# Layer 1 of a two-layer graph attention kernel: tile 29 of head 0 through logarithms, tile 28 of its sum through a DMA

## The chip, the cores and the metric

The kernel runs on one core of one Trainium2 chip. The metric is the device time of one execution in microseconds (us); the median of three executions of the kernel before is 2761.76 us (2758.8 to 2762.07).

## What is computed

Two graph layers are applied to x (4096 x 512, fp32) with one 4096 x 4096 adjacency matrix of zeros and ones. The change is in layer 1 alone:

```python
data1 = (h @ W.T + b).reshape(4096, 8, 64)         # h = relu(layernorm(x)), 8 heads of 64
src, trg = sums of data1 * src_proj, data1 * trg_proj over the 64 columns
e = src.T[:, :, None] + trg.T[:, None, :]          # 8 x 4096 x 4096
e = where(e >= 0, e, 0.01 * e) + adj
out = softmax(e, axis=-1) @ data1 (per head);  x = x + out
```

Layer 1 adds the adjacency matrix to the scores, so every pair of nodes takes part. The kernel writes a weight as max(z, g) times d times exp(adj), with a factor z of each output row and head and two factors g and d of each neighbour and head; the weights of a head, summed over the neighbours, are its softmax denominator.

## The kernel before, in words

Layer 0 and the linear part of layer 1 come first and are not touched. Layer 1's attention (lines 1232 to 1614) then runs over 8 groups: 4 blocks of 1024 output rows times 2 sets of 4 heads (k = 0 to 3). A group runs over 32 tiles m of 128 neighbours. For every tile and head a product tile `pr[i, m, k]` of 128 x 1024 is made, and TensorE multiplies it with the values.

**Products.** VectorE makes each by one scalar_tensor_tensor (L1379 for head 0, L1382 for the others; order 3, 0, 1, 2). ScalarE supplies exp(adj) once per tile (`exps`, L1319, one buffer `ex`), head 3's own factor (`last_exps`, L1329) and head 0's relu (`relus`, L1355). Tiles in `BY_LOG` are different for head 0: ScalarE writes a relu of logarithms into the single buffer `lg_row` (`logs`, L1335, four tiles ahead), GpSimd adds the adjacency tile to it in two halves (`add_logs`, L1344: the first half in the step of tile m-2, the second in that of m-1, held back behind head 3's product there), and ScalarE's exponential of it is the product itself (`relus`, L1352). VectorE then has three products for that tile in place of four. Head 0's products have three buffers in turn, those of head 3 two.

**Denominators.** Heads 1 and 2: four matmuls per tile (`den`). Head 3: GpSimd adds the products up (L1393) and TensorE sums the result over the partitions in the last tile. Head 0: each tile goes one of two ways. Those in `BY_DMA` are added by an accumulating DMA from GpSimd's queue into one of two accumulators `acc[i, 0, 0]`, `acc[i, 0, 1]` in turn (L1365; tiles 0 and 1 are copied in at L1363); the turn is counted so that tile 30 lands in the second. Those in `BY_HALF` are split: TensorE sums the left half at once by one matmul (L1447), and GpSimd adds the right half into `acc[i, 0, 2]` (L1397, L1399). In `gather` (L1401), the last tile brings in the accumulators: acc[i,0,0] and acc[i,3] right after the values of heads 3 and 0, then acc[i,0,2], and at the very end acc[i,0,1] (L1450).

**TensorE's columns.** Matmuls of layer 1 use 32 of the array's 128 columns, so that four stand side by side, one in each column group 0 to 3. A tile has 20 of them, five per column group. `n`, the number of `BY_HALF` tiles before m modulo 4, sets with which group a tile begins (`cols`), and the left half's matmul of a `BY_HALF` tile goes to group n. While a group of tiles runs, `finish` turns the results of the group before at tiles 2, 6, 10 and 14 (L1499), always beginning with column group 0.

**Order.** Each engine runs its instructions in the order in which the program text issues them; `stages` (L1596) sets how many tiles each function is ahead of `gather`. In the step of a tile, `weigh` (L1367) issues on GpSimd's queue: the DMA of the tile before (`sums`), the second half of the logarithms of tile m+1, head 3's add, the first half of the logarithms of tile m+2, and the half sum.

Of the kernel before, what the change touches and what calls it, by code (L numbers as in the profile page):

```python
# [28 lines left out]
def kernel(  # L29
# [657 lines left out]
    def slot(name):  # L687
        n = taken.get(name, 0)
        taken[name] = n + 1
        return slots[name][n % len(slots[name])]  # L690
# [544 lines left out]


    PARTS = (0, 1, 2, 4, 5, 6, 8, 9, 10, 12, 13, 14, 16, 17, 18, 22)
    BY_LOG = (3, 7, 11, 15, 19, 23, 27, 31)
    BY_HALF = (4, 8, 12, 16, 20, 24, 28)
    BY_DMA = [m for m in range(NT - 1) if m not in BY_HALF]  # L1240
    after = mybir.DependencyInfo(mybir.DependencyClass.Sync, mybir.DependencyReason.DATA)

# [3 lines left out]
    with tile_pool("rl") as rlp, tile_pool("zb") as zp1, tile_pool("ac") as acp, tile_pool("s1") as sp, tile_pool(  # L1246
# [85 lines left out]
        def logs(i, m, early=False):  # L1332
            if m in BY_LOG and early == (m == BY_LOG[0]):
                r = lg_row
                nc.scalar.activation(r, us[i], AF.Relu, bias=nlg_m[:, groups[i][1], m:m + 1], scale=-(1.0 - SLOPE))  # L1335
                rl[i, m] = r

        def early_logs(i, m):
            logs(i, m, True)

        def add_logs(i, m, half, behind=None):
            if m in BY_LOG:
                cs = slice(half * BL, (half + 1) * BL)
                add = nc.gpsimd.tensor_tensor(rl[i, m][:, cs], rl[i, m][:, cs], ra[i, m][:, cs], ALU.add)  # L1344
                if behind is not None:
                    tc.add_manual_dep(add.ins, behind.ins.name, after, reason="behind head 3's product")

        def relus(i, m):
            h = groups[i][1] * HG
            if m in BY_LOG:  # L1350
                pr[i, m, 0] = slot("pr0")
# [15 lines left out]
        def weigh(i, m, order=ORDER):  # L1367
# [26 lines left out]
            add_logs(i, m + 2, 0)  # L1394
            if m == BY_HALF[0]:
                acc[i, 0, 2] = acp.tile([P, BL], FP, name="acc02", bufs=1)
                nc.gpsimd.tensor_copy(acc[i, 0, 2], pr[i, m, 0][:, BL:])  # L1397
            elif m in BY_HALF:
                nc.gpsimd.tensor_tensor(acc[i, 0, 2], acc[i, 0, 2], pr[i, m, 0][:, BL:], ALU.add)  # L1399

        def gather(i, m):  # L1401
# [5 lines left out]
            v, dn = pv[i]  # L1407
            n = sum(u < m for u in BY_HALF) % 4
            cols = [(n + c) % 4 for c in range(4)]
# [13 lines left out]
            def ones(col, row, src, stop=False):  # L1423
                den(col, zo[:, 3 - row:4], src, start=False, stop=stop)

            def halves(src):
                return [src[:, q * BL:(q + 1) * BL] for q in range(HV)]
# [13 lines left out]
            for col in cols:  # L1441
# [3 lines left out]
                    start=(m == 0), stop=(last and r == 1))  # L1445
            if m in BY_HALF:
                ones(n, 3 if n else 1, halves(pr[i, m, 0])[0])  # L1447
# [149 lines left out]
        for s in range(len(steps)):  # L1597
            for f, ahead in stages:
                if s + ahead < len(steps):
                    f(*steps[s + ahead])  # L1600
                if s == 0 and f is exps:
                    early_logs(0, BY_LOG[0])
            if s == 0:
# [45 lines left out]
```

## Time and profile before

| | |
|---|---|
| median of three executions | 2761.76 us |
| the profiled execution | 2753.08 us, of which the profile's span is 2751.3 us |
| TensorE clock granted, mean | 0.999 |
| layer 1's attention | some 1180 us of the span; a group takes 146.4 us |

In a group of 146.4 us, TensorE is busy for all of it, VectorE for 145.7 us, GpSimd for 125.3 us and ScalarE for 120.8 us. The profile calls TensorE's matmuls PE and its weight loads PEld, VectorE DVE, ScalarE ACT, GpSimd POOL and SyncE, which loads the adjacency tiles, SP. A line "L1382 DVE ... he_t<-z,rm,ex" is an instruction of line 1382 that writes a buffer in tile he_t from z, rm and ex; buffers of layer 0 are used again under their old names, so that head 0's product is called he_t or pr, and head 3's he_t for an even tile and at for an odd one. A fp32 matmul shows as two records. "[0.40 <-DVE ...]" is idle time before an instruction and what ended it.

### The profile page before, as it was taken

Reading aid. Unit: us, or ns where it says so; the run is one execution under the profiler, and the core shown is the slowest. Engines: PE = TensorE matmul, PEld = TensorE weight load, DVE = VectorE, ACT = ScalarE, POOL = GpSimd, SP = SyncE. Lnnn points to the kernel's source line nnn. Section 1 sums busy time; section 2 is a strip of 40 time slices with the busy share of each in tenths; the row PEclk is TensorE's granted clock in tenths of the full one; section 3 lists DMA queues with packets and bytes.
Section 4 is the critical chain, followed back from the end, with each engine's and each line's share of the span. In section 5 each row is a group of like instructions: output and inputs, shape, how many; then the busy total and the mean of one; then the engine's idle time right before and its main releaser. Section 6 shows DMA issues by size and latency. Waiting matters only on the chain.

```text
span 2751.3 us, 49011 instructions
## 1 busy us (share of the span) xinstructions
PE 2733.0 (99%) x17839; PEld 1774.7 (65%) x17839; DVE 2473.0 (90%) x3362; ACT 1545.5 (56%) x2498; POOL 1454.8 (53%) x1252
## 2 busy tenths in 40 slices
PE   8999999999999999999999999999999999999999
PEld 6885444446888888888885433565656565655555
DVE  6767789899989888888886799999999999999998
ACT  6422233333133333433433588988788888888886
POOL 5313434453011011101108588988889897979797
PEclk9999999999999999999999999999999999999999
DMA  6628898888999999999866589999999999989897
GB/s 207 190 68 298 280 328 302 312 300 262 216 212 197 196 263 204 229 257 228 232 193 166 172 203 263 226 223 242 234 240 221 242 234 241 228 241 230 218 221 173
DMA packets 537122, 632.10 MB, mean 230 GB/s; under 512 B 292184, under 2 KB 346488, under 8 KB 536880
## 3 DMA queue, kind: packets, MB, share of 16 engines
q1 hardware_dynamic: 463600, 419.28, 50.5%
q0 software_dynamic: 71776, 206.81, 34.9%
q8 instruction: 140, 2.29, 0.3%
q10 hardware_dynamic: 1504, 2.88, 0.3%
q14 instruction: 102, 0.84, 0.1%
HBM read 406.33 MB, written 107.15 MB: 187 GB/s over the span
## 4 chain that ended last, share of the span: by engine, by line
PE 80%; DVE 7%; DMA 3%; issue 3%; SPq 3%; POOL 2%; ACT 2%; DVEq 0%; POOLq 0%; ACTq 0%
PE pv L1416 28%; PE po L845 21%; PE pe L585 12%; PE dn L1421 8%; PE bank L297 6%; SPq L768 2%; PE po L980 2%; DVE he_t L1382 2%; DMA et<-er_d 1%; PE pt L1499 1%; DMA a<-in_adj_t_dram 1%; POOL a L992 1%; PE bank L230 1%; PE bank L237 0%; DVE at L812 0%
## 5 line engine op out<-in xcount | busy, mean ns | idle before, releaser
L1416 PE MATMUL pv<-he_t,sup 128*32 128x512 f32 x6488 | 988.0, 592 | 1.1 <-DVE he_t L1382 1.1
L1416 PEld LDWEIGHTS pv<-he_t,sup 128*32 128x32 f32 x6488 | 434.9, 110 | 311.4 <-issue 110.7
L1421 PE MATMUL dn<-he_t,acc_z 128*2 128x512 f32 x1984 | 412.9, 592 | 0.0
L585 PE MATMUL pe<-he_t,he_t 128*128 128x512 f32 x896 | 386.2, 592 | 0.0
L802 ACT ACTIVATE d<-d 128x1024 f32<-128x1024 f32 x126 | 133.3, 1058 | 423.2 <-DVE d L794 223.4
L1319 ACT ACTIVATE ex<-he_t 128x1024 f32<-128x1024 f32 x255 | 262.3, 1029 | 148.1 <-DVE he_t L1382 147.0
L1393 POOL TENSOR_TENSOR acc<-acc,at 128x1024 f32<-128x1024 f32 x120 | 287.9, 2399 | 69.9 <-DVE at L1382 63.7
L1382 DVE SCALAR_TENSOR_TENSOR he_t<-z,rm,ex 128x1024 f32<-128x1024 f32 x256 | 315.3, 1271 | 0.5
L1382 DVE SCALAR_TENSOR_TENSOR he_t<-he_t,rm,ex 128x1024 f32<-128x1024 f32 x254 | 312.8, 1271 | 0.8 <-PE dn L1421 0.4
L585 PEld LDWEIGHTS pe<-he_t,he_t 128*128 128x128 f32 x896 | 169.3, 190 | 210.3 <-issue 193.8
L1393 POOL TENSOR_TENSOR acc<-acc,he_t 128x1024 f32<-128x1024 f32 x120 | 287.5, 2396 | 26.6 <-DVE he_t L1382 26.6
L1416 PE MATMUL pv<-at,sup 128*32 128x512 f32 x1024 | 279.7, 593 | 0.0
L845 PE MATMUL po<-sup,ux 128*128 128x256 f32 x1024 | 263.3, 379 | 0.0
L845 PE MATMUL po<-he_t,at 128*128 128x256 f32 x1024 | 263.0, 379 | 0.1
L845 PE MATMUL po<-sup,at 128*128 128x256 f32 x1024 | 242.4, 380 | 1.3 <-DVE at L812 1.1
L845 PEld LDWEIGHTS po<-sup,at 128*128 128x128 f32 x1024 | 194.0, 190 | 29.5 <-DVE at L812 3.4
L845 PEld LDWEIGHTS po<-he_t,at 128*128 128x128 f32 x1024 | 194.3, 190 | 27.3 <-ACT zs L875 0.5
L845 PEld LDWEIGHTS po<-sup,ux 128*128 128x128 f32 x1024 | 193.9, 190 | 26.1
L812 DVE TENSOR_TENSOR at<-d,a 128x1024 f32<-128x1024 f32 x126 | 154.1, 1223 | 62.7 <-PE po L845 30.9
L596 ACT ACTIVATE nr<-rm 128x1 f32<-128x1 f32 x144 | 29.3, 204 | 301.5 <-DVE rm L587 290.6
L590 POOL DMA_DIRECT2D er_d<-mk x136 | 75.3, 553 | 226.2 <-DVE rm L587 214.1
L1416 PE MATMUL pv<-pr,sup 128*32 128x512 f32 x680 | 187.7, 592 | 0.0
(349 smaller groups left out, 5345.6 us busy)
## 6 DMA issues: line engine op xcount, KB each, us to landing
he_t<-in_adj_t_dram SPq DMA_DIRECT2D x256, 512.0 KB, 6.3
acc<-he_t POOLq DMA_DIRECT2D x127, 512.0 KB, 6.8
a<-in_adj_t_dram SPq DMA_DIRECT2D x126, 512.0 KB, 5.3
acc<-pr POOLq DMA_DIRECT2D x65, 512.0 KB, 6.4
ac<-in_adj_t_dram SPq DMA_DIRECT2D x124, 256.0 KB, 4.9
ar<-in_adj_dram SPq DMA_DIRECT2D x120, 256.0 KB, 4.6
ec_d<-mc POOLq DMA_DIRECT2D x120, 256.0 KB, 5.0
er_d<-mk POOLq DMA_DIRECT2D x112, 256.0 KB, 4.5
```

The costliest lines, as they stand in the source:

```text
L297: nc.tensor.matmul(acc[:, j, :], w, m, start=(k == 0), stop=(k == KC // 2 - 1))
L585: nc.tensor.matmul(pe[:, :w], he_t[i][:, k, (t % TB) * P:(t % TB + 1) * P], he_t[j][:, k, BL - w:], start=(k == 0), stop=(k == KC - 1))
L590: nc.gpsimd.dma_start(er_d[rows, lo + sk:lo + w], mk[:, sk:w])
L768: nc.sync.dma_start(e[c * S:(c + 1) * S, h, 0:r * P].rearrange("p (a q) -> p a q", q=S), sq[c])
L802: nc.scalar.activation(d, d, AF.Exp)
L812: nc.vector.tensor_tensor(w, d, aj.pop((n, q)), ALU.mult)
L845: nc.tensor.matmul(acc[:, j, :], A[:, j * P:(j + 1) * P], B, start=(first_ and j == 0), stop=last, skip_group_check=True)
L1319: nc.scalar.activation(x_, ra.pop((i, m)), AF.Exp)
L1382: p_ = nc.vector.scalar_tensor_tensor(w, zs_[i, k], g_m[:, h + k, m:m + 1], e3.pop((i, m)) if k == 3 else x_, op0=ALU.max, op1=ALU.mult)
L1393: nc.gpsimd.tensor_tensor(acc[i, 3], acc[i, 3], w, ALU.add)
L1416: nc.tensor.matmul(v[c][q][col * Q:(col + 1) * Q, :], va[:, m, g * HG + k, c0:c0 + Q], pr[i, m, k][:, q * BL:(q + 1) * BL], start=(m == 0) ...
L1421: nc.tensor.matmul(dn[col * Q:col * Q + w.shape[1], :], w, src, **fl)
```

## The change

```diff
     PARTS = (0, 1, 2, 4, 5, 6, 8, 9, 10, 12, 13, 14, 16, 17, 18, 22)
-    BY_LOG = (3, 7, 11, 15, 19, 23, 27, 31)
-    BY_HALF = (4, 8, 12, 16, 20, 24, 28)
+    BY_LOG = (3, 7, 11, 15, 19, 23, 27, 29, 31)
+    BY_HALF = (4, 8, 12, 16, 20, 24)
     BY_DMA = [m for m in range(NT - 1) if m not in BY_HALF]
```

In each of the 8 groups, tile 29's head 0 loses VectorE's product and ScalarE's relu and gets ScalarE's relu of logarithms, two half adds on GpSimd and ScalarE's exponential. Tile 28's head 0 loses the left half's matmul on TensorE and the right half's add on GpSimd and gets an accumulating DMA of 128 x 1024. `BY_DMA` grows from 24 to 25 tiles, so the turn of the two accumulators starts the other way round: tile 2 is added to the accumulator into which tile 1 was copied, no longer to that of tile 0; from tile 27 on, tiles 28 and 30 go to the second and 27 and 29 to the first. Tiles 29 to 31 begin with TensorE's column group 2 in place of 3. In the changed program the exponentials of tiles 29 and 31 wait for the landing of a DMA besides GpSimd's halves, which that of tile 31 did not before: their buffers were last used by tiles 26 and 28, which now are both read by a DMA. No other line is changed.

## The prediction

> **What bounds the kernel now.** I read first the busy times by window, since the page's shares are means over two layers. This is a whole group of 32 tiles of layer 1, then three stretches at its end and the next one's start (columns: window, its length, busy time and instructions of each engine, granted clock, DMA share, GB/s).
>
> ```profile
> 2422.80:2569.20 146.40, 146.40 (x1477) 85.30 (x1473) 145.71 (x122) 120.75 (x142) 125.34 (x83) 1.00 0.93 234
> 2430.00:2435.00 5.00, 5.00 (x53) 3.15 (x47) 5.00 (x5) 3.35 (x4) 4.44 (x3) 1.00 0.70 265
> 2435.00:2440.00 5.00, 5.00 (x52) 3.10 (x48) 5.00 (x6) 3.39 (x4) 4.43 (x3) 1.00 0.94 195
> ...
> 2445.00:2450.00 5.00, 5.00 (x52) 3.04 (x46) 5.00 (x6) 4.43 (x7) 1.66 (x2) 1.00 1.03 376
> ```
>
> Two engines look full: TensorE with 146.40 us and VectorE with 145.71. Busy shares can't say which one sets the pace. The starts of the matmuls can (timeline of TensorE, tiles 27, 29 and 31, whose head 3 is in at):
>
> ```profile
> 2424.26 0.60 PE L1416 MATMUL pv<-at,sup 128*32 128x512 f32 x2
> ...
> 2432.85 0.60 PE L1416 MATMUL pv<-at,sup 128*32 128x512 f32 x2
> 2433.28 0.60 PE L1416 MATMUL pv<-at,sup 128*32 128x512 f32 x2
> ...
> 2441.43 0.60 PE L1416 MATMUL pv<-at,sup 128*32 128x512 f32 x2
> ```
>
> Records of one column group follow each other every 0.43 us (2432.85, 2433.28), so a matmul of two records holds its group for 0.858 us, and a tile of five per group takes 4.29 us. Tiles 29 and 30 take 2441.43 - 2432.85 = 8.58 us, exactly twice that: **TensorE runs without a gap**. The waits of five groups (who waited for whom; us in total, times, longest) say the same:
>
> ```profile
> PEld pv L1416 <- DVE he_t L1382: 2.9, 9, 0.4
> ...
> ACT he_t L1352 <- POOL lg L1344: 15.0, 26, 0.6
> ...
> DVE he_t L1382 <- PE dn L1421: 0.2, 1, 0.2
> ```
>
> TensorE waits 0.6 us per group for products, and VectorE's whole idle time is 146.4 - 145.7 = 0.7 us. VectorE's lead over TensorE is widest in the middle of a group and falls to 2441.43 - 2439.92 = 1.5 us at tile 31 (end of its head 3, below). TensorE sets the pace; VectorE is close behind.
>
> The Trainium skill's page "Perfetto Trace Analysis", section "Identifying the Most-Contended Engine", warns that matmul busy time doesn't measure how close TensorE is to its limit, and would take VectorE's occupancy of 99.5% as the bound; by it, the sum below would be VectorE's term, -3.9 to -9.5 us. The spacing of the matmuls speaks for TensorE.
>
> **The change, part by part, per group.**
>
> *TensorE: one matmul less (tile 28, column group 2).* Shared by four groups it would be 0.858 / 4 = 0.21 us, at most 0.858 us. But tiles 27 and 28, with it, took 2432.85 - 2424.26 = 8.59 us, as long as tiles 29 and 30 without. Column groups run on independently and meet again where the results are turned (tile 14) and after the last tile. In between, the half sums of tiles 16, 20, 24, 28 lie on groups 3, 0, 1, 2, and the last tile puts 2, 3, 2, 2 more matmuls on groups 0 to 3. That makes 3, 4, 3, 3; without tile 28's, 3, 4, 2, 3. Group 1 is the longest in both. I take **0**; the end for the range is 8 x -0.858 = -6.9 us.
>
> *VectorE: one product less (tile 29).* Its row is 1.27 us, from start to start 1.19 us; 8 x 1.19 = 9.5 us at most. What replaces it runs on ScalarE and GpSimd, both in order, so I walk the group's end with the timeline's rows, GpSimd's (head 3's add of tile 27, the half sum of tile 28 that goes, head 3's add of tile 31), ScalarE's (logarithms of tile 31, `ex` of tile 29) and VectorE's (tile 29's heads 3 and 0, tile 31's head 3):
>
> ```profile
> 2421.87 2.40 POOL L1393 TENSOR_TENSOR acc<-acc,at 128x1024 f32<-128x1024 f32 x1 [0.42 <-DVE at L1382]
> ...
> 2427.87 1.28 POOL L1399 TENSOR_TENSOR acc<-acc,pr 128x512 f32<-128x512 f32 x1
> ...
> 2440.08 2.40 POOL L1393 TENSOR_TENSOR acc<-acc,at 128x1024 f32<-128x1024 f32 x1 [0.45 <-DVE at L1382]
> ```
>
> ```profile
> 2427.27 1.14 ACT L1335 ACTIVATE lg<-racc,mb 128x1024 f32<-128x1024 f32 x1
> 2428.96 1.03 ACT L1319 ACTIVATE ex<-he_t 128x1024 f32<-128x1024 f32 x1 [0.55 <-DVE he_t L1382]
> ```
>
> ```profile
> 2428.85 1.39 DVE L1382 SCALAR_TENSOR_TENSOR at<-z,rm,he_t 128x1024 f32<-128x1024 f32 x1
> 2430.16 1.27 DVE L1379 SCALAR_TENSOR_TENSOR he_t<-rl,mb,ex 128x1024 f32<-128x1024 f32 x1
> ...
> 2438.60 1.32 DVE L1382 SCALAR_TENSOR_TENSOR at<-z,rm,he_t 128x1024 f32<-128x1024 f32 x1
> ```
>
> The relu of tile 29's logarithms (1.14) goes behind tile 27's exponential, where ScalarE waits 1.05 us for VectorE: free. On GpSimd, head 3's add of tile 27 ends at 2424.2; the first half (1.28) ends at 2425.5, the DMA issue (0.85) at 2426.3, the second half at 2427.6. Tile 29's exponential (1.15 for the relu's 1.23) can then start at 2427.7, not 2426.1; the relu of tile 31 follows until 2429.9 and `ex` of tile 29 runs 2429.8 to 2430.8, **0.84 us later than now**. VectorE, done with head 3 at 2430.2, waits 0.6 us for it. So of 1.19 us about **0.5 us** stays; tile 30's products start at 33.24, not 33.73. In groups 0 and 1 ScalarE also scales values (0.57 per tile) and nothing stays. All of it lies behind TensorE, which reads these products 1.5 us and more later: I take 0; the end is -9.5 us.
>
> *GpSimd:* two halves more (2 x 1.28), one less (1.28) and a DMA issue (0.85): +2.1 of 21 us of idle time. Continuing the walk: head 3's add of tile 28 ends at 2430.0, the new DMA of tile 28 is issued until 2430.8, tile 29's add ends at 33.25, tile 31's halves at 34.5 and 36.6 (now 36.5), tile 31's add at 42.2 (now 42.5). TensorE reads it at 2443.2. Hidden; uncovered it would cost what it is late.
>
> *Exponentials of tiles 29 and 31* now wait for landings of the DMAs of tiles 26 and 28. Tile 26's, issued at 2420.58, took 6.0 us, landing 2426.6, before 2427.7. Tile 28's, issued at 2430.0 with 5.6 to 7 us, lands between 2435.6 and 2437, against 2436.6 for the halves. At most 0.4 us late; ScalarE's copies of the results, for which the next group's first matmul (2447.6) waits, end at 2447.1 now and would end about 0.5 earlier. Hidden.
>
> *Tile 2's add* goes to the accumulator that tile 1 is being copied into. That copy landed 0.6 to 1.6 us after the add's issue in groups 1 to 7 (2457.91 against 2457.32 here), and GpSimd stands for that long; queued behind are head 3's add and tile 3's DMA. Three operations later GpSimd idles 1.81 us. VectorE's product of tile 5, which reuses tile 2's buffer, starts at 2466.90, and that DMA landed at 2464.39. Hidden; else up to 7 x 1.6 us.
>
> *One accumulating DMA of 512 KB more.* The window 2430 to 2435 has room (share 0.70), those after it less (0.94 to 1.03). What matters is tile 30's DMA, in TensorE's way at 2446.80: issued at 2438.79, landed at 2445.01 after 6.2 us. Over the groups this slack is 1.45 to 2.05 us. Six DMAs would now follow each other, 4.5 us apart, where there were three; the last of three at 3.6 us took 6.8 to 7.7 us. Tile 30's would land 0.3 to 1.3 us later: I take 0. The longest landing of any such DMA, 9.0 us, would be 2.8 us later: 2.8 - 1.45 = 1.35 us per group, 8 x 1.35 = +10.8 us.
>
> The skill's "DMA: Bandwidth & Descriptors", section "Anatomy of one DMA — SWDGE (gpsimd) path", fits 2.0 us plus bytes / 436e3, an estimate of 3.2 us for 512 KB, by which no landing could be late; these rows say 5.6 to 9.0, and they decide.
>
> **Sum.** 0 for all parts: 2753.1 us for the profiled execution, whose span is 2751.3. The median of the runs is 8.7 us above it, so for the median **2761.8 us**.
>
> **Rivals.**
>
> - *VectorE, or column group 2, was the bound after all* (for: 145.71 of 146.40; against: the even 4.29 us). -3.9 us (8 x 0.49) to -9.5; middle -7: 2754.8. Chance 0.14.
> - *Tile 30's DMA lands late, slower.* At a group's end, in L1450, and from 1.5 to 2.0 us later than now, that is about 8 us after issue. For: shares near 1, 8.2 to 9 us at the busiest places; against: the room before. Some 0.85 us x 8 = +7: 2769. Chance 0.20.
> - *ScalarE is held up* by tile 28's landing: beyond some 8.6 us after its issue it pushes `ex` of tile 31 (now 2438.71) and the copies behind it by more than their 1 us of slack. Likewise +7: 2769. Chance 0.08.
> - The change not saving VectorE's time is part of the forecast: 0.6 of 1.19 us comes back as a wait for `ex`.
>
> **Numbers.** No change (within 0.2%, 5.5 us, about what a measurement of this kernel can tell from none): 0.58. Faster by more: 0.14; slower by more: 0.28. The range, 2755 to 2770, takes in the nearer part of each rival and leaves out some 2 in 10.
>
> **What would show it.** Right: a group still of 146.4 us; `ex` of tile 29 waits for ScalarE's order and VectorE waits some 0.6 us for it; tiles 31 still 4.29 us each; no TensorE wait at L1421 for a DMA. Wrong: a gap in the matmuls ahead of dn<-acc, or a group under 146.0 us.

## The result and the profile after

| | before | changed |
|---|---|---|
| median of the runs, us | 2761.57 | 2781.82 (2780.38 to 2783.83) |
| ratio, 95% interval | 1 | 1.0084 (1.0072 to 1.0095) |
| profiled execution, us | 2753.08 | 2780.38 |
| groups of layer 1, us each (groups 0 to 6) | 146.3 to 147.5 | 148.6 to 151.0 |

Each median is of four executions. The changed kernel is slower by 20 us, outside the predicted range of 2755 to 2770. The two profiled spans differ by 27 us, of which some 5 us lie ahead of layer 1's attention (the value matmuls of its first tile 1 start at 1572.5 in the one and at 1577.4 in the other); the seven groups, each measured from that point to the next group's, add up to 21.6 us more. So what follows compares groups.

A whole group of the changed kernel and three stretches at the end of the group before it, with the columns of the same view of before:

```profile
2322.28:2472.01 149.73, 148.38 (x1474) 73.59 (x1470) 149.73 (x120) 121.29 (x143) 129.80 (x84) 1.00 0.93 235
2300.00:2305.00 5.00, 5.00 (x51) 2.90 (x43) 5.00 (x4) 4.97 (x5) 4.58 (x3) 1.00 0.72 186
2305.00:2310.00 5.00, 4.66 (x44) 1.14 (x40) 5.00 (x5) 2.54 (x3) 5.00 (x5) 1.00 0.99 259
2310.00:2315.00 5.00, 4.67 (x42) 1.35 (x40) 5.00 (x4) 3.98 (x4) 4.58 (x4) 1.00 0.98 243
```

VectorE has fewer instructions per group (120 for 122) and is now busy for all 149.73 us; TensorE, which was full, has 1.35 us of gaps. VectorE has less to do and takes longer, so some of its instructions must have grown. TensorE's records show where the time is lost (changed kernel, timeline of TensorE, tiles 27, 29 and 31):

```profile
2294.82 0.60 PE L1416 MATMUL pv<-at,sup 128*32 128x512 f32 x2
...
2303.43 0.62 PE L1416 MATMUL pv<-at,sup 128*32 128x512 f32 x2
...
2313.76 0.62 PE L1416 MATMUL pv<-at,sup 128*32 128x512 f32 x2
```

From 27 to 29 it is still 8.6 us, from 29 to 31 it is 10.33 in place of 8.58. The waits of five groups (who waited for whom; us in total, times, longest):

```profile
PEld pv L1416 <- DVE he_t L1382: 24.4, 39, 1.4
ACT he_t L1352 <- POOL lg L1344: 22.9, 27, 2.4
...
ACT he_t L1352 <- DMA acc<-he_t: 6.4, 2, 3.3
...
PEld dn L1421 <- DMA acc<-he_t: 4.4, 5, 1.2
...
PEld dn L1421 <- DMA acc<-pr: 1.2, 2, 0.8
```

TensorE waits 24.4 us for VectorE's products, where it was 2.9. Waits for an accumulator's DMA (rival 2) are 4.4 + 1.2 = 5.6 us in five groups; before shows none. The rest is read from three timelines of the same group's end. First GpSimd: head 3's add of tile 27, the two halves of tile 29's logarithms, head 3's add of tile 28, the new DMA of tile 28, and the same for tiles 29 to 31:

```profile
2293.23 2.38 POOL L1393 TENSOR_TENSOR acc<-acc,at 128x1024 f32<-128x1024 f32 x1 [0.44 <-DVE at L1382]
2295.58 2.26 POOL L1344 TENSOR_TENSOR lg<-lg,he_t 128x512 f32<-128x512 f32 x1
...
2298.39 1.56 POOL L1344 TENSOR_TENSOR lg<-lg,he_t 128x512 f32<-128x512 f32 x1
2299.64 2.64 POOL L1393 TENSOR_TENSOR acc<-acc,he_t 128x1024 f32<-128x1024 f32 x1
2301.97 1.14 POOL L1365 DMA_DIRECT2D acc<-he_t  x1
2303.53 2.39 POOL L1393 TENSOR_TENSOR acc<-acc,at 128x1024 f32<-128x1024 f32 x1 [0.42 <-DVE at L1382]
2305.89 2.27 POOL L1344 TENSOR_TENSOR lg<-lg,he_t 128x512 f32<-128x512 f32 x1
...
2309.96 2.65 POOL L1393 TENSOR_TENSOR acc<-acc,he_t 128x1024 f32<-128x1024 f32 x1
```

Then VectorE: head 3 of tiles 27, 28 and 29, what follows 29's, and head 3 of tile 31:

```profile
2291.73 1.34 DVE L1382 SCALAR_TENSOR_TENSOR at<-he_t,rm,he_t 128x1024 f32<-128x1024 f32 x1
...
2295.38 1.31 DVE L1382 SCALAR_TENSOR_TENSOR he_t<-he_t,rm,at 128x1024 f32<-128x1024 f32 x1
...
2300.19 3.18 DVE L1382 SCALAR_TENSOR_TENSOR at<-he_t,rm,he_t 128x1024 f32<-128x1024 f32 x1
2303.30 2.46 DVE L1382 SCALAR_TENSOR_TENSOR he_t<-he_t,rm,ex 128x1024 f32<-128x1024 f32 x2
...
2310.51 3.19 DVE L1382 SCALAR_TENSOR_TENSOR at<-he_t,rm,he_t 128x1024 f32<-128x1024 f32 x1
```

And ScalarE: tile 29's exponential and its `ex`, then tile 31's:

```profile
2299.99 1.15 ACT L1352 ACTIVATE he_t<-lg,t_m 128x1024 f32<-128x1024 f32 x1 [2.40 <-POOL lg L1344]
...
2302.23 1.01 ACT L1319 ACTIVATE ex<-he_t 128x1024 f32<-128x1024 f32 x1
...
2311.02 1.15 ACT L1352 ACTIVATE he_t<-lg,t_m 128x1024 f32<-128x1024 f32 x1 [3.13 <-DMA acc<-he_t]
2312.07 1.01 ACT L1319 ACTIVATE ex<-he_t 128x1024 f32<-128x1024 f32 x1
```

Read the three side by side. GpSimd's half starts at 2295.58, 0.2 us after head 3's product of tile 28, and takes 2.26 us, not 1.28, and GpSimd is a microsecond late from there on. Head 3's add of tile 28 starts at 2299.64, the product of tile 29 at 2300.19, in the middle of it: now the *product* takes 3.18 us, not 1.3, and ends 1 us after the add (2302.28). The same pair comes again with tiles 30 and 31. In both cases the later of the two is drawn out by about what was left of the earlier one (2296.69 - 2295.58 = 1.1 us for the half, 2302.28 - 2300.19 = 2.1 for the product). In groups 2 to 6 of before head 3's products of tiles 27 to 31 took 1.3 to 1.4 us; in the changed kernel those of tiles 29 and 31 take 3.2 us. (In groups 0 and 1 it is those of tiles 28 and 30, with 2.1 us each, and the stretch below grows by 1.2 us, not 2.5.)

From the start of tile 27's head-3 product to the end of tile 31's it is 2313.70 - 2291.73 = **21.97 us; before it was 19.51** (2439.92 - 2420.41; VectorE's head 3 of tiles 27 and 28 in before):

```profile
2420.41 1.31 DVE L1382 SCALAR_TENSOR_TENSOR at<-z,rm,he_t 128x1024 f32<-128x1024 f32 x1
...
2424.02 1.33 DVE L1382 SCALAR_TENSOR_TENSOR he_t<-z,rm,at 128x1024 f32<-128x1024 f32 x1
```

This stretch is the yardstick of the experiments. Its growth is the drawn-out products less the product that was saved: 1.8 us at tile 29 and 1.9 at tile 31, less 1.2, make 2.5.

### The profile page after: what moved, and what is told of

It is laid out like the page before. It is cut to its first block, busy times and chain, and to the rows that moved or that the text cites. A ratio compares the mean times of both kernels' runs of the same rounds, so it can differ in the third digit from the quotient of the medians.

```text
span 2778.5 us, 48977 instructions
## 1 busy us (share of the span) xinstructions
PE 2749.0 (99%) x17823; PEld 1706.6 (61%) x17823; DVE 2495.2 (90%) x3354; ACT 1550.3 (56%) x2506; POOL 1484.1 (53%) x1268
## 4 chain that ended last, share of the span: by engine, by line
PE 50%; DVE 21%; issue 9%; POOL 6%; DMA 6%; ACT 5%; SPq 2%; DVEq 0%; POOLq 0%; ACTq 0%
PE po L845 24%; DVE he_t L1382 13%; PE pe L585 12%; PE bank L297 5%; PE pv L1416 4%; DMA acc<-he_t 3%; PE po L980 2%; DVE at L1382 2%; DVE he_t L1379 2%; ACT at L1329 2%; POOL lg L1344 2%; POOL acc L1393 2%; SPq L768 1%; PE dn L1421 1%; DMA acc<-pr 1%
## 5 line engine op out<-in xcount | busy, mean ns | idle before, releaser
L1416 PE MATMUL pv<-he_t,sup 128*32 128x512 f32 x6488 | 973.5, 593 | 8.7 <-DVE he_t L1382 6.7
L1416 PEld LDWEIGHTS pv<-he_t,sup 128*32 128x32 f32 x6488 | 391.8, 110 | 360.6 <-issue 159.3
L1421 PE MATMUL dn<-he_t,acc_z 128*2 128x512 f32 x1984 | 393.3, 592 | 0.0
L1382 DVE SCALAR_TENSOR_TENSOR he_t<-z,rm,ex 128x1024 f32<-128x1024 f32 x256 | 315.1, 1270 | 1.8 <-ACT ex L1319 1.8
L1382 DVE SCALAR_TENSOR_TENSOR he_t<-he_t,rm,ex 128x1024 f32<-128x1024 f32 x254 | 312.6, 1270 | 1.4 <-ACT ex L1319 1.4
L1416 PE MATMUL pv<-at,sup 128*32 128x512 f32 x1024 | 275.4, 593 | 0.0
L1344 POOL TENSOR_TENSOR lg<-lg,he_t 128x512 f32<-128x512 f32 x144 | 200.0, 1389 | 24.1 <-DVE he_t L1382 24.1
```

Of the source, the lines that this page charges most:

```text
L1382: p_ = nc.vector.scalar_tensor_tensor(w, zs_[i, k], g_m[:, h + k, m:m + 1], e3.pop((i, m)) if k == 3 else x_, op0=ALU.max, op1=ALU.mult)
L1416: nc.tensor.matmul(v[c][q][col * Q:(col + 1) * Q, :], va[:, m, g * HG + k, c0:c0 + Q], pr[i, m, k][:, q * BL:(q + 1) * BL], start=(m == 0) ...
L1421: nc.tensor.matmul(dn[col * Q:col * Q + w.shape[1], :], w, src, **fl)
```

## The experiments

The theories, with the letters used in the expectations. *A*: VectorE's head-3 product, the only one with two inputs in SBUF (z and `e3`; the others read `ex` in PSUM), and a GpSimd operation that reads SBUF hold each other up, and the drawn-out products are the loss. *B*: the loss is the landing of tile 28's DMA, for which tile 31's exponential waits (rival 3). *C* or *F*: it is the turn of the two accumulators at tile 2. *Q*: GpSimd's added time in its queue, whatever VectorE reads. *G*, formed later: A and Q together.

All ratios are to the kernel before, with a 95% interval.

### The two halves of the change by themselves

```diff
-    BY_LOG = (3, 7, 11, 15, 19, 23, 27, 31)
+    BY_LOG = (3, 7, 11, 15, 19, 23, 27, 29, 31)
     BY_HALF = (4, 8, 12, 16, 20, 24, 28)
```

> Before with the ninth tile of logs (29), tile 28 still split in halves: no DMA more, the turn of the accumulators and the wait of tile 31's exponential as before. GpSimd gets 2 x 1.28 us more per group and loses nothing. Theory A (GpSimd falls behind in tiles 27 to 31, and its adds then run beside VectorE's head 3 product, which reads two SBUF tiles and is stretched from 1.3 to 3.2 us): ratio to before 1.006 or more, stretched products at tiles 29 and 31 in every group. Theory B (ScalarE's exponential of tile 31 waits for the landing of tile 28's DMA): 1.000, that wait is gone. Theory C (tile 2's add waits for tile 1's copy): 1.000.

Measured: **1.0084** (1.0069 to 1.0099), yardstick 23.2 us. Head 3's product takes 4.4 us at tile 29 and 3.2 at tile 31 (3.0 + 1.9 - 1.2 = 3.7, the growth of the yardstick), and no exponential there waits for a DMA.

```diff
     BY_LOG = (3, 7, 11, 15, 19, 23, 27, 31)
-    BY_HALF = (4, 8, 12, 16, 20, 24, 28)
+    BY_HALF = (4, 8, 12, 16, 20, 24)
```

> Before with tile 28 summed by DMA, no ninth tile of logs: GpSimd has 0.4 us less to do per group; tile 31's exponential waits for tile 28's landing and tile 2's add for tile 1's copy. Theory A: 1.000 to 1.001, no stretched product at tiles 29 and 31. Theory B: most of the loss stays, 1.005 to 1.008, with ScalarE waiting up to 3 us at tile 31. Theory C: some 1.002, with a stretched product at tile 4 in some groups.

Measured: **1.0011** (1.0001 to 1.002), yardstick 19.4 us, no drawn-out product in tiles 28 to 31. The loss belongs to the ninth tile of logarithms; tile 28's DMA and the turn cost some tenth of a per cent, at the edge of what can be told from none.

### Less work for GpSimd, and no landing of tile 28

```diff
-            elif m > 1:
+            elif m > 1 and m not in (28, 30):
                 nc.gpsimd.tensor_tensor(acc[i, 3], acc[i, 3], w, ALU.add)
```

> The changed kernel with GpSimd's adds of head 3 left out for tiles 28 and 30 (head 3's denominators lack these tiles), which gives GpSimd 4.8 us per group. Theory A: no product stretched at tiles 29 and 31, ratio 0.999 to 1.002. Theories B and C: 1.006 to 1.008, as the DMAs and their waits are the same.

Measured: **1.0031** (1.0022 to 1.004), more than A's forecast, yardstick 20.0 us. Nothing is drawn out at tiles 29 and 31 any more, but the loss isn't all gone: VectorE now waits 1.83 us for `ex` at tile 29, since the half adds ahead of it are as late as before.

```diff
-            elif m in BY_DMA:
+            elif m in BY_DMA and m != 28:
```

> The changed kernel without the accumulating DMA of tile 28 (head 0's denominators lack this tile): no wait of tile 31's exponential for a landing, 0.85 us less on GpSimd's queue, one transfer less. Theory A: the product of tile 29 still meets the add of tile 28, so at least one stretched product per group (some 2.2 to 3.2 us) stays: 1.003 to 1.006. Theory B: 1.000 to 1.002.

Measured: **1.0087** (1.0072 to 1.0102), yardstick 22.0 us, products of tiles 29 and 31 still 3.2 us. Tile 31's exponential waits 2.40 us for GpSimd's half where it waited for the DMA. By itself theory B falls; A's forecast of 1.003 to 1.006 was missed too, since two products of each group stayed drawn out.

### The mechanism without the kernel

Six loops of VectorE's product and GpSimd instructions, each between two barriers; the two that matter:

```python
for _ in range(12):
    nc.vector.scalar_tensor_tensor(w, z, g, second, op0=ALU.max, op1=ALU.mult)   # second: e (SBUF) or q (PSUM)
for _ in range(8):
    nc.gpsimd.tensor_tensor(acc, acc, pr, ALU.add)
```

> The whole computation is left out; six stretches of VectorE's product (128x1024) and GpSimd instructions are run by themselves: product with two SBUF inputs alone; GpSimd's add alone; both together; product with its second input in PSUM beside the add; two SBUF inputs beside GpSimd memsets; two SBUF inputs beside GpSimd's accumulating DMAs. Theory A (a product with two SBUF inputs and a GpSimd operation that reads SBUF exclude each other): alone 1.2 to 1.4 us and 2.4 us; together products rise to 3 to 3.7 us where an add is under way, and the adds too, so that 8 adds and 12 products take about 8 x 2.4 + 12 x 1.2 = 33.6 us instead of the longer of 19.2 and 14.4; with PSUM 1.2 to 1.4 us and 2.4 us as alone; beside memsets as alone. Theory D (GpSimd and VectorE slow each other whatever they read): the PSUM stretch and the memset stretch are drawn out too. Theory E (the DMA issue is what stands in the way): only the last stretch is drawn out.

VectorE's timeline (start, length, count at the end: 8 products alone; 12 beside adds; 12 with PSUM beside adds; 12 beside memsets; 12 beside accumulating DMAs) and GpSimd's (4 adds alone; 8 beside two SBUF inputs; 8 beside PSUM; 8 memsets):

```profile
6.32 10.53 DVE L73 SCALAR_TENSOR_TENSOR w<-z,g,e 128x1024 f32<-128x1024 f32 x8 [4.17 <-DMA e<-in_adj_dram]
...
27.46 31.62 DVE L73 SCALAR_TENSOR_TENSOR w<-z,g,e 128x1024 f32<-128x1024 f32 x12
...
59.53 15.76 DVE L73 SCALAR_TENSOR_TENSOR w<-z,g,q 128x1024 f32<-128x1024 f32 x12
...
79.44 15.81 DVE L73 SCALAR_TENSOR_TENSOR w<-z,g,e 128x1024 f32<-128x1024 f32 x12
...
95.71 15.80 DVE L73 SCALAR_TENSOR_TENSOR w<-z,g,e 128x1024 f32<-128x1024 f32 x12
```

```profile
17.61 9.59 POOL L80 TENSOR_TENSOR acc<-acc,pr 128x1024 f32<-128x1024 f32 x4
...
28.75 25.29 POOL L85 TENSOR_TENSOR acc<-acc,pr 128x1024 f32<-128x1024 f32 x8
...
59.84 19.34 POOL L90 TENSOR_TENSOR acc<-acc,pr 128x1024 f32<-128x1024 f32 x8
...
80.71 8.01 POOL L95 MEMSET mm<- 128x1024 f32 x8
```

Alone, a product takes 10.53 / 8 = 1.32 us and an add 9.59 / 4 = 2.40. One after the other, 12 products and 8 adds would be 15.8 + 19.2 = 35.0 us; side by side without hindrance, 19.2. They take 31.62: nearly one after the other. With the second input in PSUM (15.76 and 19.34), beside GpSimd memsets (15.81), and beside GpSimd's accumulating DMAs (15.80) a product is as fast as alone. That the two hold each other up stands; that it carries the loss is another matter.

### The turn of the accumulators

```diff
-                acc[i, 0, m] = acp.tile([P, WL], FP, name=f"acc0{m}", bufs=1)
-                nc.gpsimd.dma_start(acc[i, 0, m], pr[i, m, 0])
+                n = (len(BY_DMA) + m) % 2
+                acc[i, 0, n] = acp.tile([P, WL], FP, name=f"acc0{n}", bufs=1)
+                nc.gpsimd.dma_start(acc[i, 0, n], pr[i, m, 0])
```

> The changed kernel, but tile 2's sum goes to the accumulator of tile 0's copy again, as before the change (tiles 0 and 1 are copied in the other way round). Theory A: only tile 4's drawn-out product goes, at most 1.9 us in some groups: 2772 to 2782 us (ratio 1.004 to 1.008), and the products of tiles 29 and 31 stay at 3.2 us. Theory F (the loss comes from the turn of the accumulators): back to 2762 to 2765.

> Tile 28's sum by DMA alone (no ninth tile of logarithms), with tiles 0 and 1 copied in the other way round, so that tile 2's sum follows tile 0's copy. Theory A: GpSimd has 1.28 us less to read and nothing takes its place, and tile 4's product is not drawn out: 2758 to 2763 us (ratio 0.999 to 1.000), against 1.001 with the turn as the change has it. Theory F: the same; theory of the DMA engines (one transfer more costs time): 1.001 or more.

Measured: the changed kernel with this edit **1.007** (1.0055 to 1.0085), products of tiles 29 and 31 still 3.2 us; with eight tiles of logarithms and this edit **1.0009** (1.000 to 1.0019), against 1.0011 without it. The turn can't be told from nothing in the second pair, and is at most a small part in the first; F falls. What it does is seen in the changed kernel's trace, GpSimd and then VectorE, tiles 1 to 4 of a group:

```profile
2325.87 0.58 POOL L1363 DMA_DIRECT2D acc<-pr  x1
...
2333.16 0.89 POOL L1365 DMA_DIRECT2D acc<-he_t  x1 [2.43 <-DVE he_t L1382]
2333.79 2.67 POOL L1393 TENSOR_TENSOR acc<-acc,at 128x1024 f32<-128x1024 f32 x1
```

```profile
2334.39 3.16 DVE L1382 SCALAR_TENSOR_TENSOR he_t<-z,rm,at 128x1024 f32<-128x1024 f32 x1
```

Tile 2's add stands for 2.43 us until tile 1's copy has landed (the profile names VectorE, but that product was long done; the DMA landed at 2332.61). Tile 3's add is late behind it and draws out the product of tile 4 (2.0 to 3.8 us in groups 1 and 3 to 6). That seems to have a price of its own, though a small one: in the profile of the kernel with tile 28's DMA alone, this product takes 1.5, 3.1, 2.0, 2.2 and 1.4 us in groups 2 to 6, and these groups take 146.5, 147.6, 146.9, 147.0 and 146.4 us.

### PSUM in place of the second SBUF input

```diff
-                    p_ = nc.vector.scalar_tensor_tensor(w, zs_[i, k], g_m[:, h + k, m:m + 1],
-                                                        e3.pop((i, m)) if k == 3 else x_,
+                    y = e3.pop((i, m)) if k == 3 else x_
+                    if k == 3 and i and m in (29, 31):
+                        y = last_pt[0].rearrange("p j h d -> p (j h d)").unsqueeze(1).to_broadcast([P, 2, BL])
+                    ... scalar_tensor_tensor(w, zs_[i, k], g_m[:, h + k, m:m + 1], y,
```

(The diff is shortened.)

> The changed kernel, but in groups 1 to 7 head 3's products of tiles 29 and 31 read their second input from PSUM (an old 128x512 buffer, taken twice) in place of head 3's exponential in SBUF, which is still computed; so head 3's weights of these two tiles are other numbers. GpSimd does all that it does in the changed kernel. Theory A (two SBUF inputs against GpSimd's reads): the products of tiles 29 and 31 stay at 1.3 us, GpSimd's half at 2.3 us falls to 1.3, and what is left is groups 0 and tile 4: 2762 to 2768 us (ratio 1.000 to 1.002). Theory Q (GpSimd's added time in its queue is the loss, whatever VectorE reads) and theory C (the turn): 2779 to 2782.

Measured: **1.0077** (1.0058 to 1.0097). The products of tiles 29 and 31 are back at 1.27 us, yet next to nothing is gained: **A in this narrow form, that these two products are the loss, falls.** VectorE's timeline (tile 29's head 3 and what follows), then ScalarE's (exponentials of tiles 29 and 31) and GpSimd's (first half of tile 29):

```profile
2309.65 1.27 DVE L1386 SCALAR_TENSOR_TENSOR at<-he_t,rm,pt 128x1024 f32<-128x1024 f32 x1
2312.75 2.47 DVE L1390 SCALAR_TENSOR_TENSOR he_t<-he_t,rm,ex 128x1024 f32<-128x1024 f32 x2 [1.83 <-ACT ex L1319]
```

```profile
2309.47 1.15 ACT L1352 ACTIVATE he_t<-lg,t_m 128x1024 f32<-128x1024 f32 x1 [2.44 <-POOL lg L1344]
...
2320.77 1.15 ACT L1352 ACTIVATE he_t<-lg,t_m 128x1024 f32<-128x1024 f32 x1 [3.41 <-DMA acc<-he_t]
```

```profile
2305.03 2.26 POOL L1344 TENSOR_TENSOR lg<-lg,he_t 128x512 f32<-128x512 f32 x1
```

VectorE waits 1.83 us for `ex`, just what the drawn-out product took too much. In the changed kernel that wait lay under the drawn-out product: `ex` of tile 29 was ready at 2303.24, the product done at 2303.37. Two delays, equally long and side by side, both behind the same late half adds; taking one away shows the other. At tile 31 the exponential now waits for the landing of tile 28's DMA.

The run does not take the mutual hindrance itself away. The products of tiles 28 and 30 still read two SBUF inputs: tile 28's draws the first half out to 2.26 us, where the expectation had 1.3, which makes the wait for `ex` longer by a microsecond, and tile 30's now takes 2.2 us itself. No run here gives all five products of the stretch a PSUM input, so how much of the loss the hindrance carries and how much the plain lateness of GpSimd is not separated by this run. (The prediction's walk had that lateness without the hindrance, and came to a wait of 0.6 us and no loss.)

### More work for GpSimd that reads nothing

```diff
+        scr = rlp.tile([P, 384], FP, name="scr")      # and, in tiles 27 and 28 of each group:
+            for _ in range(4):
+                nc.gpsimd.memset(scr, 0.0)
```

(The diff is shortened.)

> The kernel before with eight GpSimd memsets of 128x384 more per group, four behind head 3's add of tile 27 and four before that of tile 28: at 1.0 us for 128x1024 (measured beside VectorE's products) some 3.0 us more of GpSimd's time, which only writes; the ninth tile of logarithms alone brings 2.6 us, which reads. Theory A: no product is drawn out; ratio 0.999 to 1.001. Theory Q: as the ninth tile alone, 1.007 to 1.010.

Measured: **1.0081** (1.0064 to 1.0098), yardstick 22.5 us: against A, for Q. Yet the way is A's again, in GpSimd's timeline and VectorE's:

```profile
2300.39 2.13 POOL L1364 MEMSET scr<- 128x384 f32 x4
2302.49 2.39 POOL L1401 TENSOR_TENSOR acc<-acc,he_t 128x1024 f32<-128x1024 f32 x1
```

```profile
2302.52 3.45 DVE L1388 SCALAR_TENSOR_TENSOR at<-he_t,rm,he_t 128x1024 f32<-128x1024 f32 x1
...
2309.47 2.31 DVE L1388 SCALAR_TENSOR_TENSOR he_t<-he_t,rm,at 128x1024 f32<-128x1024 f32 x1
```

The memsets hold nobody up themselves (0.5 us each, where 0.4 was reckoned); they push tile 28's add behind them until it starts 0.03 us ahead of tile 29's product, which then takes 3.45 us. Tile 30's product, with 2.31 us, meets a read as well. The two lose 2.1 + 0.9 = 3.0 us, which is all that the yardstick grew by. So here time on GpSimd's queue that reads nothing cost as much as reads did, because it ended in such meetings.

That gave **theory G**: the products of head 3 and GpSimd's reads are one queue. In the yardstick of the changed kernel that queue holds five products of 1.31, four adds of 2.40 and four halves of 1.28: 6.6 + 9.6 + 5.1 = 21.3 us of its 21.97. In before it held two halves and the half sum: 6.6 + 9.6 + 3 x 1.28 = 20.0, against 19.51: it was full already, with products and adds overlapping by 0.2 or 0.3 us at their ends. And the change takes the product of tile 29's head 0 from VectorE, so that the time between two head-3 products, in which GpSimd can read, shrinks there from 3.5 us (2430.24 to 2433.73) to 2.3 (2303.37 to 2305.68), which tile 29's add alone fills.

### The overfull queue relieved, in steps

```diff
-            if m in BY_LOG:
+            if m in BY_LOG and m != 29:                          # first kernel
+            if m in BY_LOG and m != 29 and (m, half) != (31, 0):    # second kernel
                 cs = slice(half * BL, (half + 1) * BL)
```

> The changed kernel without GpSimd's two half adds of tile 29 (its head-0 weights lack the adjacency); all else stays, the ninth relu and exponential on ScalarE and tile 28's DMA too. Theory G (GpSimd's reads must fit between head 3's products): behind tile 27 only head 3's add is left, which fits; behind tile 29, a tile of logarithms, the add and the first half of tile 31 (2.40 + 1.28 = 3.7 us) still meet 2.4 us. So one drawn-out product is left, at tile 31 and not at tile 29; from tile 27's head-3 product to the end of tile 31's it takes about 19.5 - 1.2 + 1.9 = 20.2 us (before 19.5, changed 22.0), and the ratio is 1.001 to 1.004. A theory in which ScalarE's order or tile 28's landing carries the loss: 1.007 to 1.009.

> The changed kernel without GpSimd's two half adds of tile 29 and the first of tile 31 (the head-0 weights of these lack the adjacency there). Theory G: nothing is left that does not fit; no product is drawn out, the stretch takes about 18.3 us, and the ratio is 0.999 to 1.001 (tile 28's DMA and tile 2's turn keep their part; TensorE sets the pace). If tile 28's landing carries a loss of its own, ScalarE waits for it at tile 31's exponential by more than 1 us, and the ratio stays at 1.003 or more.

> The changed kernel with PSUM as second input of head 3's products at tiles 29 and 31 (groups 1 to 7), and without tile 28's DMA (head 0's denominators lack it). With PSUM inputs alone VectorE waited 1.83 us for exp(adj) at tile 29 and up to 0.75 us at tile 31, the latter behind tile 28's landing. If both count, the second wait goes and the ratio falls from 1.0077 to 1.004 to 1.006; if only GpSimd's lateness counts (tile 29's exponential 2.4 us late), it stays at 1.007 to 1.008.

Measured: without tile 29's halves **1.0038** (1.0025 to 1.0051), yardstick 20.1 us in three of five groups (2 to 6) and 19.4 in two; without the three halves **1.0011** (1.0001 to 1.0021), yardstick 18.2 to 18.6 us; with PSUM inputs and without tile 28's DMA **1.0047** (1.0032 to 1.0062), 20.1 us. The first is as G had it, the second lies at the edge of it, and the third is within the forecast that counts both waits. VectorE in the first of them, head 3 of tiles 29 and 31:

```profile
2299.94 1.27 DVE L1382 SCALAR_TENSOR_TENSOR at<-he_t,rm,he_t 128x1024 f32<-128x1024 f32 x1
...
2308.35 3.24 DVE L1382 SCALAR_TENSOR_TENSOR at<-he_t,rm,he_t 128x1024 f32<-128x1024 f32 x1
```

Tile 29's is well again, tile 31's is not, because tile 31's first half still falls behind tile 29's add (in the two groups with 19.4 us it is tile 30's product that is drawn out, to 2.1 and 2.3 us). In the second kernel GpSimd has room once more (its add of tile 29, timeline): the relu and the exponential of the ninth tile and tile 28's DMA are all still there.

```profile
2295.71 2.39 POOL L1393 TENSOR_TENSOR acc<-acc,at 128x1024 f32<-128x1024 f32 x1 [1.57 <-DVE at L1382]
```

So the step from 1.0084 to 1.0011 is GpSimd's three half adds; the 0.001 left is as much as that of the kernel with tile 28's DMA alone. (TensorE's waits for VectorE's products, `PEld pv L1416 <- DVE he_t L1382`, still add up to 24.1 us in five groups of the second kernel's profile, as in the changed kernel: that sum is no measure of the loss.) The third kernel may show what is left of theory B: with the products of tiles 29 and 31 well again, leaving out tile 28's DMA gains some 1.0077 - 1.0047 = 0.003; with them drawn out it gained nothing (1.0087 without it). The intervals just overlap, and with the DMA its issue of 0.85 us leaves GpSimd's queue too, so that tile 30's product falls from 2.2 us to 1.4; whether it was the landing is not shown.

### Two tries at a better kernel

```diff
-    BY_HALF = (4, 8, 12, 16, 20, 24, 28)
+    BY_LOG_1 = (2, 5, 8, 11, 15, 19, 23, 27, 31)      # groups 1 to 7
+    BY_HALF = (12, 16, 20, 24, 28)
```

> Nine tiles of logarithms in groups 1 to 7, placed so that no half add falls into the step of another tile of logarithms: 2, 5, 8, 11, 15, 19, 23, 27, 31 (group 0 keeps its eight), and five tiles with a half sum (12, 16, 20, 24, 28), so that 26 go by DMA. From the start of tile 27's head-3 product to the end of tile 31's, GpSimd's reads are those of the kernel before. Theory G (VectorE's head-3 products and GpSimd's reads form one queue, and the change overfilled it in tiles 27 to 31): that stretch is 19.5 us again, no product is drawn out; VectorE has 144.5 us of work per group, TensorE two matmuls less than before (tiles 4 and 8): 2752 to 2763 us (ratio 0.996 to 1.000). A ninth tile costs by itself, wherever it stands (GpSimd's sum per group, or VectorE and ScalarE in lockstep): 1.005 to 1.009. The DMAs are the limit (two more than before): 1.002 or more, with waits for landings.

> The same with the matmuls of the turn beginning with the tile's own column group (which differs from group 0 at tile 14 alone here). Theory G with TensorE setting the pace: 0 to 0.2 us per group below the run with nine spread tiles, ratio 0.995 to 1.000; if the turn's order alone brought the 0.001 measured for it, 0.001 below that run.

Measured: **1.005** (1.0033 to 1.0067), and with the turn's order **1.0051** (1.0036 to 1.0066). The yardstick is 19.5 us as G foretold, but the forecast of the time fell, and what was measured lies at the lower end of "a ninth tile costs by itself": VectorE now waits for `ex` elsewhere, 18.5 us in five groups (before: 1.8), above all at tiles 6 and 11, where ScalarE also scales the results of the group before. ScalarE's exponential of tile 11 stands for a landing:

```profile
2367.98 1.15 ACT L1356 ACTIVATE he_t<-lg,t_m 128x1024 f32<-128x1024 f32 x1 [3.02 <-DMA acc<-he_t]
```

A fitting end of the group is not enough for a ninth tile; whether any place for it is cheap was not found out.

```diff
-                for c0 in range(0, P, Q):
+                for c0 in [(n + col) % 4 * Q for col in range(4)]:      # n = t // 2
                     nc.tensor.matmul(p2[c0:c0 + Q, :, :].rearrange("p k d -> p (k d)"),
```

> The kernel before; only the matmuls that turn the results at tiles 2, 6, 10 and 14 begin with the column group with which their tile begins (0, 1, 2, 3) in place of group 0. If TensorE's column groups set the pace of the kernel before and are aligned anew at each turn, each of the three later turns costs up to 0.6 us less: up to 1.8 us per group, 7 x 1.8 = 12.6 us: 2749 to 2760 us (ratio 0.995 to 0.999). If VectorE, at 145.7 of 146.4 us, is next in line right behind, at most 7 x 0.7 = 5 us: 0.998. If the turns do not align the groups: 1.000.

Measured: **0.9989** (0.9978 to 0.9999), the only kernel here that is below the one before, by some 3 us at the most likely. Groups 3 to 6 of its profile take 145.9 us each, where those of before take 146.4; one of them (columns as above):

```profile
2178.77:2324.69 145.92, 145.92 (x1481) 53.69 (x1476) 145.54 (x122) 120.68 (x143) 125.20 (x82) 1.00 0.94 235
```

The group is 0.5 us shorter, not 1.8. An edit of TensorE's order alone made it so: TensorE did set the pace of the kernel before. That VectorE, with 145.54 us of work in 145.92, is what stops the rest is likely, not shown.

## Why the prediction was wrong

**What bounds the kernel before: right.** TensorE's columns set the pace, as the last experiment shows, with VectorE close behind; rival 1 did not come, since neither the change nor a part of it was faster.

**TensorE's term, taken as 0: right; VectorE's: left open.** With tile 28's matmul taken out alone and the turn undone, the ratio is 1.0009 and groups 3 to 6 take 146.5 to 146.6 us. For the missing product there is the kernel without the three half adds, at 1.0011; but in its groups 2 to 6 the product of tile 4 or 5 is drawn out to 2.7 to 4.1 us, which may hide a gain.

**The step that failed: "+2.1 of 21 us of idle time ... Hidden".** GpSimd's idle time was no room, for two reasons that its rows in before show. It lies elsewhere: in the yardstick's 19.5 us GpSimd idles for 2.8 us of the group's 21. And it lies under head 3's products: 13 of the 21 us, and 2.2 of these 2.8, are time in which such a product runs, as here for tile 29 (2428.85 to 2430.24):

```profile
2430.38 2.40 POOL L1393 TENSOR_TENSOR acc<-acc,at 128x1024 f32<-128x1024 f32 x1 [1.23 <-DVE at L1382]
```

A read that is put there draws the product out or is drawn out itself. What was left for reads in the stretch was 0.6 us, and 1.28 us of reads net went in there. The lines shown in the prediction had the sign of it: each "[0.42 <-DVE at L1382]" is an add that waits for the product that it reads. It is a data wait, and I took the time behind it for slack; but the product is running in it.

**The walk of the group's end used fixed durations.** It put tile 29's first half at 2424.2 to 2425.5, just where head 3's product of tile 28 runs (2424.02 to 2425.35, the row of before shown above), and left it at 1.28 us. Its start held: with the head-3 products of tile 28 laid over each other (2295.38 on 2424.02), the first half starts at 2424.22, where the walk had 2424.2. Then the half takes 2.26 us, not 1.28. Tile 29's exponential starts at 2428.6 (walk 2427.7), its `ex` at 2430.9 (2429.8), and head 3's product of tile 29, which the walk let end at 2430.2, ends at 2432.0. Tile 30's head 3 starts at 2434.3 (2433.24); tile 31's ends at 2442.3, 2.4 us later than before. VectorE's lead over TensorE there was 1.5 us. The walk's "0.84 us later" for `ex` was right in kind and less than half the size (1.9); "about 0.5 us stays" of VectorE's 1.19 became a loss of 2.4.

**"Hidden; uncovered it would cost what it is late"** was the place for this case, without a price. What uncovers it is that a product meeting an add loses 1.9 us at once: the first half is 1 us late, and the product behind it nearly two.

**Landings.** Tile 28's DMA took 8.9 us (issued 2301.97, landed 2310.91), where the walk had 5.6 to 7, and beyond the 8.6 us of rival 3, and tile 31's exponential did wait for it. But a GpSimd half ended 0.6 us earlier and the drawn-out product later, so it decided nothing: without tile 28's sum the ratio stays at 1.0087. Rival 2, tile 30's landing at the group's end, shows as a wait of TensorE of 5.6 us over five groups, 1.1 in each; it is not the loss either, since with the ninth tile alone these waits are 0.9 us in all and the ratio is the same 1.0084.

**Tile 2's add, "hidden"**: it stands for 2.4 us, not 1.6, and its lateness draws out a product of tile 4. Undone, the ratio went from 1.0084 to 1.007; with intervals that overlap, a gain is likely and not shown.

None of the three rivals was this one: that an engine with a seventh of its time idle is full at one place, since its reads and VectorE's head-3 products nearly exclude each other.

## What to carry to other kernels

Idle time of GpSimd is room for reads of SBUF only where VectorE isn't running an operation with two inputs in SBUF; before work is added to GpSimd, add such VectorE operations and GpSimd's reads up as one queue, tile by tile, and note that a product saved on VectorE shortens the time in which GpSimd can read. When a drawn-out instruction is found, take it away before blaming it: here an equal wait lay under it, and only relieving what made both late gave the time back.

## What the runs showed of the hardware

VectorE's scalar_tensor_tensor of 128x1024 fp32 with two SBUF inputs (1.32 us alone) and GpSimd's tensor_tensor add (2.40 us alone) take 31.62 us for 12 and 8 of them together, 90% of the 35.0 us one after the other; with one input in PSUM, or beside GpSimd's memsets and DMA issues, there is no such effect.

The Trainium skill's page "SBUF — State Buffer", section "Who interferes with whom", states this rule: a VectorE instruction with two SBUF inputs contends with a GpSimd instruction that reads SBUF, not with one that only writes it, and the order of issue decides who blocks. It was not weighed in the prediction. The traces agree in kind (half 2.26 us when the product was first, product 3.18 when the add was first). The page says "fully blocks" of VectorE's 2-port modes; for the two-input reads here, some 10% overlapped.

The order in which the four column groups are served is worth time of its own: beginning the turn with the group with which the tile begins, in place of group 0, took 0.5 us from groups of 146.4 (145.9 in groups 3 to 6).
